# Field loads of a pairwise product kernel, divided between two queues and chosen DMA engines

## Chip, cores and metric

The kernel runs on one core of a Trainium2 chip. The metric is the device time in microseconds (us) of one execution. A core has five engines that matter here: TensorE (PE, matrix products; its weight loads are shown as PEld), VectorE (DVE), ScalarE (ACT), GpSimd (POOL) and SyncE (SP), which only issues transfers. Transfers between the chip's memory (HBM) and the core's own memory are carried out by 16 DMA engines. They are issued by SyncE, ScalarE or GpSimd, each on a queue of its own.

## Reference

There are 32 fields of 128 numbers for each of 1024 samples. For each of the 496 pairs of fields i < j, the vector of field i is multiplied by a 128 x 128 matrix of the pair's own, and the product is multiplied element by element with the vector of field j. All is in 32-bit floats.

```python
v_i = inputs[:, I_IDX, :]                       # (1024, 496, 128)
v_j = inputs[:, J_IDX, :]
transformed = jnp.einsum('bpd,ped->bpe', v_i, W)   # W: (496, 128, 128)
return transformed * v_j
```

The inputs are 16.8 MB of fields and 32.5 MB of matrices, the output is 260 MB.

## Kernel before

The host lays the fields out as `xt[128, 32, 1024]` (one row per component) and the matrices as `wt[62, 128, 8, 128]`, eight pairs to a 512 KB piece. A step `u` is one half (512 samples) of one pair `q`. Pairs go by falling i, so that the first ones need few fields. For the first 15 pairs TensorE multiplies the 32-bit floats as they are; for all later ones both factors are split into three parts (high, low, a difference), made by ScalarE and GpSimd, and three faster products are added. VectorE multiplies the result in PSUM by field j and writes it into an output tile `ot` of four pairs (2 MB), of which there are three.

```python
def load_x(f, n=1, pieces=1, eng=None):
    ...
        t = xpool.tile([P, n, BT], F32, tag=f"x{f}", name=f"x_{f}")   # one buffer per field
    ...
        (eng or nc.sync).dma_start(out=t[:, :, k * s : (k + 1) * s], in_=xt[:, f : f + n, k * s : (k + 1) * s])

def split_w(c, u):                    # two pairs' matrices
    ...
    nc.scalar.mul(h, raw, 1.0 - 2.0**-13)                               # wh, ScalarE
    nc.gpsimd.tensor_tensor(l, raw, h.bitcast(F32), ALU.subtract)       # wl
    nc.gpsimd.tensor_scalar(d, h.bitcast(F32), EPS, 1.0, ALU.mult, ALU.mult)
    nc.gpsimd.tensor_tensor(d, l.bitcast(F32), d.bitcast(F32), ALU.subtract)   # wd

# split_x does the same for half a field (xh, xl, xd)

# before the loop: matrices 0 to 2 and fields 31 to 24 are loaded
load_w(0, (0, 1, WL), nc.sync)
load_x(NF - 2, pieces=2, eng=nc.scalar)
load_x(NF - 1, pieces=2, eng=nc.scalar)
load_x(NF - 3)
load_x(NF - 4)
load_w(1, eng=nc.sync)
for f in range(NF - 5, NF - 4 - XLEAD, -1):
    load_x(f)
load_w(2, eng=nc.sync)
...
for u in range(2 * NQ + LAG + SLAG):
    q = u // 2
    if u < 2 * NQ:
        i, j = pairs[q]
        if u % 2 == 0 and j == i + 1 and 0 < i - 2 - XLEAD:
            load_x(i - 2 - XLEAD)              # at the first pair of field i: field i - 7
        first(u)                               # two products, ScalarE scales
        if u % 2 == 1 and q in w_at:
            load_w(w_at[q])
        if u == 2 * x_at + 1:
            load_x(0)
    if LAG <= u < 2 * NQ + LAG:
        second(u - LAG)                        # third product, VectorE writes ot
    while stores and stores[0][0] <= u - LAG:
        nc.scalar.dma_start(*stores.pop(0)[1:])
    ...                                        # split_w, split_x when due
```

Each engine works through its instructions in the order in which they are written here. Fields 23 to 1 are loaded inside the loop, all of them by SyncE.

Of the kernel before, what the change touches and what calls it, by code (L numbers as in the profile page):

```python
# [7 lines left out]
F32 = mybir.dt.float32  # L8
# [3 lines left out]
P = 128  # L12
NF = 32
NQ = NF * (NF - 1) // 2
BT = 1024
# [10 lines left out]
WLEAD = 12  # L26
XAFTER = 54
XLEAD = 5
SLAG = 2


# [6 lines left out]
def kernel(  # L38
# [22 lines left out]
    nc = tc.nc  # L61
# [3 lines left out]
    xpool = ctx.enter_context(tc.tile_pool(name="x", bufs=1))  # L65
# [6 lines left out]
    x_sb = {}  # L72

    def load_x(f, n=1, pieces=1, eng=None):

        if f == 0:

            t = rpool.tile([P, WL, P], F32, tag="w", name="x_0").rearrange("p q e -> p (q e)").unsqueeze(1)
        else:
            t = xpool.tile([P, n, BT], F32, tag=f"x{f}", name=f"x_{f}")  # L80
        s = BT // pieces
        for k in range(pieces):
            (eng or nc.sync).dma_start(out=t[:, :, k * s : (k + 1) * s], in_=xt[:, f : f + n, k * s : (k + 1) * s])
        for k in range(n):
            x_sb[f + k] = t[:, k, :]

    w_raw = {}

    def load_w(c, splits=(0, WL), eng=nc.sync):
        w_raw[c] = rpool.tile([P, WL, P], F32, tag="w", name=f"w_{c}")  # L90
        for a, b in zip(splits, splits[1:]):
            eng.dma_start(out=w_raw[c][:, a:b, :], in_=wt[c, :, a:b, :])
# [42 lines left out]
            todo.append((first_q[i + 1] + 1 if i < NF - 3 - NATIVE else 2, first_q[i], lambda u, i=i, a=a: split_x(i, a, u)))  # L135
    todo.sort(key=lambda t: t[1])

    load_w(0, (0, 1, WL), nc.sync)
    load_x(NF - 2, pieces=2, eng=nc.scalar)
    load_x(NF - 1, pieces=2, eng=nc.scalar)  # L140
# [8 lines that stand above are left out]
# [13 lines left out]
    def first(u):  # L162
        q, h = divmod(u, 2)
        i, c = pairs[q][0], q // WC
        r = slice(q % WC * P, (q % WC + 1) * P)
        s = slice(h * HB, (h + 1) * HB)
        po[u] = ppool.tile([P, HB], F32, tag="po", name=f"po_{u}")
        if q < nq0:
            nc.tensor.matmul(po[u], w_raw[q // WL][:, q % WL, :], x_sb[i][:, s], start=True, stop=True)  # L169
        else:  # L170
            for t in (0, 1):
                nc.tensor.matmul(po[u], w_s[c][t][:, r], x_s[i][t][:, s], start=t == 0, stop=t == 1)  # L172
            nc.scalar.mul(po[u], po[u], 1.0 + EPS)  # L173

    def second(u):
        q, h = divmod(u, 2)
        i, j = pairs[q]
        r = slice(q % WC * P, (q % WC + 1) * P)
        s = slice(h * HB, (h + 1) * HB)
        if q >= nq0:  # L180
            nc.tensor.matmul(  # L181
                po[u], w_s[q // WC][2][:, r], x_s[i][2][:, s], start=False, stop=True, skip_group_check=True
            )
        g, k = divmod(q, OG)
        if k == 0 and h == 0:
            ots[g] = opool.tile([P, OG, BT], F32, tag="ot", name=f"ot_{g}")
        nc.vector.tensor_tensor(ots[g][:, k, s], po.pop(u), x_sb[j][:, s], ALU.mult)  # L187
        if q >= NQ - 2:
            stores.append((u + SLAG, out[g, :, k, s], ots[g][:, k, s]))
        elif g == 0 or q >= NQ - OG:  # L190
            if h == 1:
                stores.append((u + SLAG, out[g, :, k], ots[g][:, k]))
        elif k == OG - 1 and h == 1:
            stores.append((u + SLAG, out[g], ots[g]))

    for u in range(2 * NQ + LAG + SLAG):
        q = u // 2
        if u < 2 * NQ:
            i, j = pairs[q]
            if u % 2 == 0 and j == i + 1 and 0 < i - 2 - XLEAD:  # L200
                load_x(i - 2 - XLEAD)
            first(u)
            if u % 2 == 1 and q in w_at:
                load_w(w_at[q])
# [3 lines that stand above are left out]
            second(u - LAG)  # L208
        while stores and stores[0][0] <= u - LAG:
            nc.scalar.dma_start(*stores.pop(0)[1:])  # L210
        if u % 2 == 1:
            ready = [t for t in todo if t[0] <= q]
            if ready:
                ready[0][2](u)
                todo.remove(ready[0])
        while later and later[0][0] <= u:
            nc.vector.tensor_tensor(*later.pop(0)[1:], ALU.subtract)  # L217
    assert not todo and not later and not stores


# [25 lines left out]
```

## Time and profile before

| | |
|---|---|
| time, median of 3 runs | 755.02 us (754.97 to 755.28) |
| span of the profiled execution | 753.2 us |
| stores, 2 MB each | 122, 12.5 us from issue to landing |
| matrix loads, 512 KB each | 61, 10.3 us |
| field loads by SyncE, 512 KB each | 30, 16.0 us |
| HBM read, written | 49.28 MB, 260.05 MB |

A page of the profile begins with the busy time of each engine and its share of the span, and the number of its instructions. Then come 40 equal slices of the span; the row DMA is the mean busy share of the 16 DMA engines in tenths, and GB/s is what they moved. For each queue the page has packets, MB and the time of its packets as a share of 16 engines' span. A row of a group of instructions has line, engine, operation, what it writes and reads, the count, then busy us and mean ns of one, then the idle time of the engine before them and what ended it. A row of waits reads: engine and line, what it waited for, us in total, times, longest us. The trace has besides every DMA packet with start, duration and size, though not the DMA engine that carried it, and the time of every increment of a transfer's semaphore, sixteen for each transfer.

### The profile page before, as it was taken

To read this page: it belongs to the slowest core of one execution; us is meant where nothing else is said; L and a number is where in the kernel's file an instruction comes from. 1 tells how busy PE (TensorE), PEld (TensorE's weight loads), DVE (VectorE), ACT (ScalarE), POOL (GpSimd) and SP (SyncE) were. 2 spreads that over 40 slices of the span, in tenths; PEclk is the share of its full clock that TensorE was granted. 3 is DMA by queue.
4 is the path that set the end of the run, shared out by engine and by line. 5 is a ranking of instruction groups with operands and counts; after the bars stand their busy time and mean duration, and the time that the engine had idled before them with its cause. 6 is when DMAs were issued, how large, how long until landed. Compare 5 with 4: busy or idle time off the path is not lost.

```text
span 753.2 us, 10948 instructions
## 1 busy us (share of the span) xinstructions
PE 706.5 (94%) x2946; PEld 546.0 (72%) x2946; DVE 624.1 (83%) x1012; ACT 627.1 (83%) x1256; POOL 595.5 (79%) x863
## 2 busy tenths in 40 slices
PE   7989999999999999999999999999999999999993
PEld 3567776777777777777777778777777777777782
DVE  4989888888887878888878897988888889888894
ACT  1389888889988898888888889898989898988892
POOL 1788998888988987978879797888887879796660
PEclk9999999999999999999999999999999999999997
DMA  9999999999999999999999999999999999999997
GB/s 353 428 427 423 430 427 424 423 417 433 399 425 406 411 420 413 415 405 401 425 401 422 412 401 422 400 432 405 417 419 421 399 432 401 425 406 413 425 397 312
DMA packets 33038, 310.04 MB, mean 412 GB/s; under 512 B 3665, under 2 KB 3793, under 8 KB 17361
## 3 DMA queue, kind: packets, MB, share of 16 engines
q10 hardware_dynamic: 19584, 261.10, 82.5%
q1 hardware_dynamic: 13392, 48.24, 16.8%
q8 instruction: 24, 0.39, 0.2%
q14 instruction: 38, 0.30, 0.1%
HBM read 49.28 MB, written 260.05 MB: 411 GB/s over the span
## 4 chain that ended last, share of the span: by engine, by line
DMA 43%; PE 32%; DVE 13%; POOL 6%; ACT 2%; issue 2%; DVEq 0%; ACTq 0%; POOLq 0%
DMA out_dram<-ot 42%; PE po L172 19%; DVE ot L187 12%; PE po L181 9%; PE po L169 4%; ACT po L173 2%; POOL xd L122 2%; POOL wl L102 1%; POOL xl L117 1%; POOL wd L104 1%; ACT wh L101 1%; POOL xl L118 1%; POOL wd L103 0%; DVE xd L217 0%; DMA x<-in_xt_dram 0%
## 5 line engine op out<-in xcount | busy, mean ns | idle before, releaser
L187 DVE TENSOR_TENSOR ot<-po,x 128x512 f32<-128x512 f32 x992 | 610.1, 682 | 118.5 <-DMA out_dram<-ot 50.7
L173 ACT ACTIVATE po<-po 128x512 f32<-128x512 f32 x962 | 543.4, 583 | 94.3 <-PE po L172 41.0
L172 PE MATMUL po<-xh,wh 128*128 128x512 f32 x962 | 382.8, 398 | 21.4 <-DVE ot L187 20.5
L172 PE MATMUL po<-xl,wl 128*128 128x512 f32 x962 | 376.6, 392 | 4.8 <-POOL wl L102 4.8
L181 PE MATMUL po<-xd,wd 128*128 128x512 f32 x962 | 375.2, 390 | 4.0 <-DVE xd L217 3.4
L172 PEld LDWEIGHTS po<-xh,wh 128*128 128x128 f32 x962 | 180.4, 188 | 88.8 <-DVE ot L187 50.8
L102 POOL TENSOR_TENSOR wl<-w,wh 128x256 fp32r<-128x256 f32 x241 | 178.3, 740 | 73.3 <-ACT wh L101 71.8
L181 PEld LDWEIGHTS po<-xd,wd 128*128 128x128 f32 x962 | 180.6, 188 | 44.0 <-ACT po L173 4.7
L172 PEld LDWEIGHTS po<-xl,wl 128*128 128x128 f32 x962 | 180.7, 188 | 42.2 <-POOL wl L102 8.8
L104 POOL TENSOR_TENSOR wd<-wl,wd 128x256 fp32r<-128x256 f32 x241 | 180.5, 749 | 20.1
L103 POOL TENSOR_SCALAR wd<-wh 128x256 fp32r<-128x256 f32 x241 | 101.3, 420 | 20.3
L101 ACT ACTIVATE wh<-w 128x256 fp32r<-128x256 f32 x241 | 99.5, 413 | 5.1 <-DVE ot L187 3.3
L117 POOL TENSOR_TENSOR xl<-x,xh 128x512 fp32r<-128x512 f32 x52 | 67.2, 1292 | 18.1 <-ACT xh L116 17.7
L122 POOL TENSOR_TENSOR xd<-xh,xl 128x512 fp32r<-128x512 f32 x32 | 41.4, 1294 | 2.7
L116 ACT ACTIVATE xh<-x 128x512 fp32r<-128x512 f32 x52 | 32.5, 629 | 11.3 <-DMA x<-in_xt_dram 11.2
L118 POOL TENSOR_SCALAR xl<-xl 128x512 fp32r<-128x512 f32 x52 | 33.7, 649 | 4.6
L169 PE MATMUL po<-x,w 128*128 128x512 f32 x60 | 27.8, 623 | 4.4 <-DMA x<-in_xt_dram 4.3
L169 PEld LDWEIGHTS po<-x,w 128*128 128x128 f32 x60 | 11.6, 198 | 19.8 <-issue 12.3
L217 DVE TENSOR_TENSOR xd<-xh,xl 128x512 fp32r<-128x512 f32 x20 | 17.2, 859 | 0.0
L116 ACT ACT_TABLE_LOAD x1 | 1.3, 1283 | 2.6 <-issue 2.6
L233 POOL MEMSET const-float32-0.0<- 128x1 f32 x1 | 0.1, 98 | 0.2 <-issue 0.2
L233 POOL MEMSET const-bfloat16-1.0<- 128x1 bf16 x1 | 0.1, 101 | 0.0
(2 smaller groups left out, 0.2 us busy)
## 6 DMA issues: line engine op xcount, KB each, us to landing
out_dram<-ot ACTq DMA_DIRECT2D x122, 2048.0 KB, 12.5
w<-in_wt_dram SPq DMA_DIRECT2D x61, 512.0 KB, 10.3
x<-in_xt_dram SPq DMA_DIRECT2D x30, 512.0 KB, 16.0
out_dram<-ot ACTq DMA_DIRECT2D x6, 512.0 KB, 9.2
x<-in_xt_dram ACTq DMA_DIRECT2D x4, 256.0 KB, 5.9
out_dram<-ot ACTq DMA_DIRECT2D x4, 256.0 KB, 8.2
w<-in_wt_dram SPq DMA_DIRECT2D x1, 448.0 KB, 4.7
w<-in_wt_dram SPq DMA_DIRECT2D x1, 64.0 KB, 2.9
```

The lines of the kernel that those rows point to most:

```text
L101: nc.scalar.mul(h, raw, 1.0 - 2.0**-13)
L102: nc.gpsimd.tensor_tensor(l, raw, h.bitcast(F32), ALU.subtract)
L103: nc.gpsimd.tensor_scalar(d, h.bitcast(F32), EPS, 1.0, ALU.mult, ALU.mult)
L104: nc.gpsimd.tensor_tensor(d, l.bitcast(F32), d.bitcast(F32), ALU.subtract)
L117: nc.gpsimd.tensor_tensor(l, x_sb[f][:, s], h.bitcast(F32), ALU.subtract)
L118: nc.gpsimd.tensor_scalar(l, l.bitcast(F32), 1.0 / EPS, 1.0, ALU.mult, ALU.mult)
L122: nc.gpsimd.tensor_tensor(d, h.bitcast(F32), l.bitcast(F32), ALU.subtract)
L169: nc.tensor.matmul(po[u], w_raw[q // WL][:, q % WL, :], x_sb[i][:, s], start=True, stop=True)
L172: nc.tensor.matmul(po[u], w_s[c][t][:, r], x_s[i][t][:, s], start=t == 0, stop=t == 1)
L173: nc.scalar.mul(po[u], po[u], 1.0 + EPS)
L181: nc.tensor.matmul(po[u], w_s[q // WC][2][:, r], x_s[i][2][:, s], start=False, stop=True, skip_group_check=True)
L187: nc.vector.tensor_tensor(ots[g][:, k, s], po.pop(u), x_sb[j][:, s], ALU.mult)
```

## The change

Fields 23 to 1 are no longer loaded by one transfer of SyncE over all 16 DMA engines. GpSimd issues a transfer of 104 rows, arranged so that it falls on 13 DMA engines with 8 rows each; SyncE issues the other 24 rows, arranged for two engines (odd fields) or twelve (even fields). The host reorders the rows of these fields to suit. Small transfers into a tile `mark`, which nothing reads, move the position at which GpSimd's next transfer begins: one of four engines at the start, one of three after each field (13 + 3 = 16), one of twelve at the end. The aim is to choose which DMA engines carry the later fields, so that some carry fewer of them. The scratch memory for GpSimd's descriptors grows from 256 to 2048.

```diff
+XROWS = 104
+BY_TWO = range(1, NF - 3 - XLEAD, 2)
...
+    mark = xpool.tile([32, 16], F32, tag="mark", name="mark")
+
+    def move_on(k):
+        nc.gpsimd.dma_start(out=mark[: 2 * k], in_=xt[: 2 * k, 0, :16].rearrange("(b a) n -> a b n", a=k))
+
+    def load_x_apart(f):
+        t = xpool.tile([P, BT], F32, tag=f"x{f}", name=f"x_{f}")
+        nc.gpsimd.dma_start(out=t[:XROWS], in_=xt[:XROWS, f, :].rearrange("(b a) n -> a b n", a=13))
+        rest = xt[XROWS:, f, :]
+        if f in BY_TWO:
+            rest = rest.rearrange("(b a) n -> a b n", a=2)
+        nc.sync.dma_start(out=t[XROWS:], in_=rest)
+        x_sb[f] = t
+        move_on(3)
...
+    move_on(4)
     load_w(0, (0, 1, WL), nc.sync)
...
             if u % 2 == 0 and j == i + 1 and 0 < i - 2 - XLEAD:
-                load_x(i - 2 - XLEAD)
+                load_x_apart(i - 2 - XLEAD)
...
             nc.vector.tensor_tensor(*later.pop(0)[1:], ALU.subtract)
+    move_on(12)
...
+    for f in range(1, NF - 3 - XLEAD):
+        xt[:XROWS, f] = xt[:XROWS, f].reshape(13, 8, BT).transpose(1, 0, 2).reshape(XROWS, BT).copy()
+        if f in BY_TWO:
+            xt[XROWS:, f] = xt[XROWS:, f].reshape(2, 12, BT).transpose(1, 0, 2).reshape(P - XROWS, BT).copy()
...
-    nc = _bacc.Bacc("TRN2", ..., dynamic_dma_scratch_size=256)
+    nc = _bacc.Bacc("TRN2", ..., dynamic_dma_scratch_size=2048)
```

More of the change, by code (lines that the diff above doesn't have):

```diff
@@ L230 @@
     xt = _np.ascontiguousarray(x.transpose(2, 1, 0))
+    for f in range(1, NF - 3 - XLEAD):
+        xt[:XROWS, f] = xt[:XROWS, f].reshape(13, 8, BT).transpose(1, 0, 2).reshape(XROWS, BT).copy()
+        if f in BY_TWO:
+            xt[XROWS:, f] = xt[XROWS:, f].reshape(2, 12, BT).transpose(1, 0, 2).reshape(P - XROWS, BT).copy()
     wt = _np.ascontiguousarray(w[perm].reshape(NQ // WL, WL, P, P).transpose(0, 3, 1, 2))
-    nc = _bacc.Bacc("TRN2", target_bir_lowering=False, num_devices=1, dynamic_dma_scratch_size=256)
+    nc = _bacc.Bacc("TRN2", target_bir_lowering=False, num_devices=1, dynamic_dma_scratch_size=2048)
     arrays, args = {}, []
```

## Prediction

> **What bounds the kernel now.** I read the page first: busy shares, then the slices and the queues.
>
> ```profile
> span 753.2 us, 10948 instructions
> PE 706.5 (94%) x2946; PEld 546.0 (72%) x2946; DVE 624.1 (83%) x1012; ACT 627.1 (83%) x1256; POOL 595.5 (79%) x863
> ...
> DMA  9999999999999999999999999999999999999997
> GB/s 353 428 427 423 430 427 424 423 417 433 399 425 406 411 420 413 415 405 401 425 401 422 412 401 422 400 432 405 417 419 421 399 432 401 425 406 413 425 397 312
> ...
> q10 hardware_dynamic: 19584, 261.10, 82.5%
> q1 hardware_dynamic: 13392, 48.24, 16.8%
> ```
>
> PE has the highest share, but the DMA row is full in every slice but the last. 310 MB are moved, 261 MB of them by the queue of ScalarE (the stores) and 48 MB by that of SyncE (weights and fields). The speed is the thing to see: about 427 GB/s in slices 1 to 9 (20 to 190 us), then mostly 400 to 425. The windows say the same:
>
> ```profile
> core 0: us, PE busy (x) PEld busy (x) DVE busy (x) ACT busy (x) POOL busy (x), PEclk, DMA share, GB/s
> 40.00:100.00 60.00, 54.98 (x234) 42.88 (x233) 52.62 (x84) 52.14 (x107) 53.67 (x73) 1.00 1.01 427
> 100.00:140.00 40.00, 37.11 (x154) 27.94 (x155) 33.78 (x56) 33.44 (x70) 35.47 (x50) 1.00 1.01 427
> 140.00:200.00 60.00, 57.09 (x241) 44.23 (x240) 51.65 (x85) 51.70 (x106) 51.88 (x75) 1.00 1.01 414
> ...
> 320.00:384.00 64.00, 60.89 (x260) 47.96 (x260) 52.68 (x88) 55.72 (x112) 53.26 (x79) 1.00 1.00 407
> ```
>
> The engines are all busy, yet they move less after 140 us. The packet records say why. A 16 KB packet takes 611 ns in 13,398 of 15,616 cases, and the next one starts 4 ns before it ends: 16384 B / 607 ns = 27.0 GB/s, times 16 = 432 GB/s, so the first 140 us run at the ceiling. The sixteen semaphore increments of each store show the rest. In the stores issued from 15 to 60 us the fifteenth comes 12.26 us after issue and the sixteenth 12.59 (medians). From 384 to 740 us the eighth comes after 7.5 us, the fifteenth after 8.8, the sixteenth after 12.0. One engine of sixteen is late. Following packets back from those last increments gives an engine that never pauses and whose 16 KB packets take 635 ns in the mean and 4 KB packets 168 instead of 159: 4% slower than its neighbours. It falls behind until the three output buffers are used up, at about 140 us, and from there sets the pace. Its neighbours then show stretched packets (up to over 1 us); counted above 611 and 159 ns they come to 8.3 us per engine from 140 to 384 us and 10.9 from 384 to 740. I take most of this as neighbours run dry and starting again.
>
> The waits name the same buffers, and one more line matters for this change:
>
> ```profile
> POOL wl L102 <- ACT wh L101: 71.8, 99, 2.8
> PEld po L172 <- DVE ot L187: 50.8, 79, 1.2
> DVE ot L187 <- DMA out_dram<-ot: 50.7, 58, 1.8
> ...
> PEld po L172 <- POOL wl L102: 8.8, 10, 1.2
> ```
>
> DVE waits 50.7 us for a store to free its buffer, nearly all after 140 us. GpSimd's 79% hides a tight first half. Its groups from 60 to 100 us:
>
> ```profile
> L104 POOL TENSOR_TENSOR wd<-wl,wd 128x256 fp32r<-128x256 f32 x13 | 10.1, 773 | 1.1
> L102 POOL TENSOR_TENSOR wl<-w,wh 128x256 fp32r<-128x256 f32 x13 | 9.9, 763 | 0.5
> L117 POOL TENSOR_TENSOR xl<-x,xh 128x512 fp32r<-128x512 f32 x6 | 7.8, 1297 | 0.0
> L103 POOL TENSOR_SCALAR wd<-wh 128x256 fp32r<-128x256 f32 x13 | 6.4, 493 | 1.1
> L118 POOL TENSOR_SCALAR xl<-xl 128x512 fp32r<-128x512 f32 x6 | 4.3, 713 | 0.5
> ```
>
> The idle column is only the 80 ns between two instructions: it waits for nothing. Gaps over 0.12 us sum to 5.6 us from 20 to 60, to 0 from 60 to 120, and to 18.7 us from 140 to 384. The split weights are ready only 0.3 to 5.9 us before TensorE wants them (0.8 us near 102).
>
> **What the Trainium skill says.** "DMA: Bandwidth & Descriptors", section "Latency and other measured facts", says that DMA engines 7 and 15 are usually slower than the others, with a cause only guessed. The trace before agrees that one engine is slower, by 4%; it doesn't tell its number. The same page, "Why a DMA increments its semaphore by 16 and not by 1": a transfer uses the largest k up to 16 that divides the outer sizes of both sides; SyncE's and ScalarE's transfers take the k lowest engines, GpSimd's take k consecutive ones from a cursor that goes round, and GpSimd's transfers post an increment from all 16 engines whatever their k. No run yet shows GpSimd's part, as the kernel before issues nothing from it. The first section gives about 1 us to the first byte of a GpSimd transfer against 0.6 from SyncE. "Perfetto Trace Analysis", "DMA Instruction — SWDGE (GPSIMD)": the descriptors are written by GpSimd's own processors, so the issue is time on POOL; not shown by this trace either.
>
> **The change part by part.** 23 fields (23 down to 1), each 512 KB, or 8 rows of 4 KB per engine, are loaded apart.
>
> Rows per engine. Before: 23 x 8 = 184. GpSimd's 104 rows are 13 engines x 8. The first mark (four engines) and each mark of three move the cursor so that the same three engines are always left out. SyncE's 24 rows go to two engines (12 rows each, 12 odd fields) or twelve (2 rows each, 11 even fields): 166 rows on the two lowest engines, 22 on the next ten. The plan adds up if the two lowest and the slow engine are the three left out: then the slow one has 0 or 22 rows, the two 166, those with both shares 206, the rest 184. The slow engine loses 162 to 184 packets x 164 ns = 27 to 30 us; nine or ten others gain 22 x 155 ns = 3.4 us.
>
> But fields are loaded only in the first half: the last of the 23 was issued at 379 us. From 140 to 384 us the neighbours' 8.3 us can come back, less the 3.4: -5. From 384 on the slow engine has its full load again: 63 stores x 8 x 631 ns + 33 loads x 8 x 164 ns = 318 + 43 = 361 us, which is what that part takes now. It starts that part without its lag, and the lag (3 us behind the fifteenth engine, 4.5 behind the eighth) is all that is won there: about -5. So at best -10.
>
> What GpSimd pays. Per field two issues: I estimate 1.0 us for 104 rows and 0.7 for the small mark, from the skill's 1 us to first byte. At 1.7 us per field:
> - Up to 60 us: some seven fields, 12 us, of which the first three fall into its idle 15 us at the start. The other four cost 7, against 5.6 of room. All marks write one tile, so each waits for the one before to land, whose increments stand behind 8 field packets per engine: 8 x (611 + 159 + 159) = 7.4 us when the queues are full. The fields from 20 down follow each other after 2 to 6 us of GpSimd's work, so I add up to 8 us of waiting there. Less 4 us of lead: PE loses about 5.
> - 60 to 140: five fields, 8.5 us, and no room: +8.
> - DMA meanwhile works off the field loads that are queued (they land 20 us after issue there), worth -4 later.
> - 140 to 384: eleven fields x 1.7 = 18.7 us, all the room there is. GpSimd then bounds this part, and the 5 us of relief are not collected: 0.
>
> Sum: +5 + 8 - 4 + 0 - 5 = +4. With some chance that the marks cost less than this, 755.0 + 3 = 758 us.
>
> **The rivals.** (1) The issues are cheap, say 0.4 us a field: GpSimd keeps its room, DMA stays the bound, and both reliefs come: 755 - 10 + 2 = about 747. For it: the first half is bound by DMA on every view. Against: 60 to 120 us has no gap at all. (2) The issues are dear, 2.5 us a field: 23 x 0.8 us more than assumed, 18 us, in parts where GpSimd has no room: about 776. (3) The position is not where the plan wants it. If the three left out are 1, 2 and 3, engine 0 gets 184 + 166 = 350 rows, 166 x 155 ns = 26 us more, in the first half alone: a new straggler, some 15 us after the lag that the buffers absorb, about 770. Against it: 13 + 3 and the two lowest engines fit too well to be unmeasured. (4) The loads were hidden anyway and GpSimd has slack elsewhere: no change, 755.
>
> **Range and chances.** The main number is one I have no measurement of, GpSimd's time per issue: 0.1 us per field is 1.5 to 2 us of the whole. From rival 1 to rival 2 gives 746 to 775. Faster by over 2% would be under 740, more than both reliefs together: 0.02. Slower by over 2% is over 770, rivals 2 and 3: 0.14. The rest: 0.84.
>
> **What would show it.** Right: issue instructions on POOL of 0.7 to 1 us, 47 in all; PE waiting for POOL's wl or wd between 30 and 140 us; the sixteenth increment of stores beside the fifteenth up to 384 us, and 3 us late again from about 540; DVE's wait for stores below 50.7 us. Wrong: if issues are short, POOL's waits for ACT stay and the time falls under 750. If another engine trails in the first half, the position was missed. If the late engine trails as before although it has no field rows, my reading of the lag is wrong.

## Result and profile after

The changed kernel takes 780.5 us in the median of 6 runs (778.7 to 781.6), the kernel before 755.0 (755.0 to 755.3): ratio 1.0334, 95% interval 1.032 to 1.0349. The prediction was 758 with a range of 746 to 775: it missed by 22 us, and the time lies outside its range.

The page of the kernel after, the same rows as were shown of before:

```profile
span 777.5 us, 11026 instructions
...
PE 709.9 (91%) x2946; PEld 551.7 (71%) x2946; DVE 643.0 (83%) x1012; ACT 627.8 (81%) x1256; POOL 623.5 (80%) x911
...
DMA  9979999999999999999999999999999999999998
GB/s 280 371 298 391 376 357 422 388 425 413 402 390 408 417 418 418 424 416 411 402 411 400 382 411 412 399 425 400 428 394 431 418 409 418 419 407 410 414 408 330
...
q10 hardware_dynamic: 19584, 261.10, 80.9%
q1 hardware_dynamic: 10788, 38.44, 13.6%
q0 software_dynamic: 4112, 9.82, 3.9%
```

GpSimd's queue q0 has taken 9.8 MB from SyncE's q1. The loss is at the start: the first six slices move 280, 371, 298, 391, 376 and 357 GB/s, where before had 353 and then 423 to 430. The windows sharpen it (columns as in the prediction). Those of after:

```profile
0.00:20.00 20.00, 14.34 (x25) 5.74 (x26) 6.85 (x12) 1.28 (x1) 3.20 (x9) 1.00 0.92 284
20.00:40.00 20.00, 17.26 (x41) 7.23 (x39) 12.39 (x20) 4.83 (x10) 13.41 (x16) 1.00 1.02 374
40.00:60.00 20.00, 12.96 (x48) 10.20 (x49) 11.63 (x19) 9.97 (x20) 11.33 (x19) 0.75 0.78 290
...
100.00:140.00 40.00, 34.99 (x150) 27.67 (x150) 36.83 (x55) 33.09 (x67) 37.12 (x54) 1.00 0.98 385
140.00:200.00 60.00, 55.93 (x242) 44.56 (x240) 56.07 (x88) 52.88 (x108) 55.62 (x79) 1.00 1.01 414
320.00:384.00 64.00, 60.63 (x257) 47.24 (x256) 51.35 (x85) 55.17 (x111) 55.61 (x82) 1.00 1.01 413
```

And those of the first 60 us of before:

```profile
0.00:20.00 20.00, 15.63 (x33) 6.43 (x34) 9.83 (x15) 4.00 (x6) 4.12 (x8) 1.00 0.91 356
20.00:40.00 20.00, 20.00 (x65) 11.91 (x64) 18.63 (x29) 7.86 (x17) 15.00 (x22) 1.00 1.03 428
40.00:60.00 20.00, 17.38 (x73) 13.18 (x72) 16.64 (x27) 16.25 (x34) 16.76 (x23) 1.00 1.01 426
```

In the first 40 us the transfers are busy (0.92 and 1.02) and yet move less: packets are stretched. From 40 to 60 us they are not even busy (0.78): TensorE works 12.96 us in place of 17.38, and little is there to store. So two different things happen.

I compare kernels below by **delay**: the start of VectorE's product of step u, less its start in the kernel before. For after it is 6.7 us at step 20 (27 us into the span of before), 14.1 at step 30, 14.0 at 40, 18.4 at 80 (74 us), 18.7 at 160 (137 us), 22.6 at 480 (378 us), 23.9 at 560 and 25.3 at the end. So 18 of the 25 us are lost before 92 us of after's own span, about five between 137 and 437 us, and nothing is won back later.

Waits of the kernel after (engine and line, what it waited for, total us, times, longest):

```profile
DVE ot L211 <- DMA out_dram<-ot: 54.9, 49, 2.8
PEld po L196 <- POOL wl L125: 41.4, 27, 7.1
...
PE po L196 <- POOL wl L125: 30.8, 23, 6.8
...
POOL mark L99 <- DMA mark<-in_xt_dram: 21.6, 5, 8.1
ACT xh L139 <- DMA x<-in_xt_dram: 18.1, 2, 17.3
```

TensorE's weight loads now wait 41.4 us for GpSimd's `wl`, where they waited 8.8. GpSimd waits 21.6 us for its own marks. VectorE waits for the stores a little longer than before (54.9 against 50.7), where a relief of the slow engine should have shortened this. The timeline of GpSimd shows the worst of the marks (start, duration, instruction, idle time before it):

```profile
36.24 0.64 POOL L104 DMA_DIRECT2D x<-in_xt_dram  x1
44.96 0.56 POOL L99 DMA_DIRECT2D mark<-in_xt_dram  x1 [8.08 <-DMA mark<-in_xt_dram]
45.53 0.73 POOL L125 TENSOR_TENSOR wl<-w,wh 128x256 fp32r<-128x256 f32 x1
```

and that of TensorE takes it over:

```profile
46.32 0.79 PE L196 MATMUL po<-xl,wl 128*128 128x512 f32 x1 [6.75 <-POOL wl L125]
```

The mark could not be issued until the mark before it had landed. `wl` stood behind it in GpSimd's order, and TensorE behind `wl`. Last, GpSimd's groups from 60 to 100 us, with the two kinds of issue:

```profile
L125 POOL TENSOR_TENSOR wl<-w,wh 128x256 fp32r<-128x256 f32 x12 | 9.4, 781 | 0.5
...
L104 POOL DMA_DIRECT2D x<-in_xt_dram x3 | 1.9, 638 | 0.0
L99 POOL DMA_DIRECT2D mark<-in_xt_dram x3 | 1.7, 567 | 0.0
```

638 + 567 ns, 1.2 us per field, where I had put 1.7.

Each store posts sixteen semaphore increments. Medians in us after the issue of the 8th, the 15th and the 16th, and the median of how far the last trails the one before, worked out from the trace:

```
stores issued from   before                   after
60 to 140 us         10.5  12.0  13.2  1.4     8.1   9.2  10.2  0.7
140 to 260            8.4   9.8  12.9  3.0     9.4  10.5  11.3  0.3
260 to 384            8.2  10.5  13.0  2.5     8.3  12.0  12.4  0.4
430 to 500            7.8   8.9  11.6  2.6     7.5   9.6  11.9  2.2
500 to 740            7.4   8.6  12.0  3.2     7.6   9.2  11.9  2.9
```

The 16th stands beside the 15th up to 384 us, as the prediction asked. But from 140 us on the 15th has become later, which a slow engine that has been relieved doesn't explain: another engine trails too.

### The profile page after: what moved, and what is told of

Its sections match the earlier page's. It is cut to its first block, busy times and chain, and to the rows that moved or that the text cites. A ratio compares the mean times of both kernels' runs of the same rounds, so it can differ in the third digit from the quotient of the medians.

```text
span 777.5 us, 11026 instructions
## 1 busy us (share of the span) xinstructions
PE 709.9 (91%) x2946; PEld 551.7 (71%) x2946; DVE 643.0 (83%) x1012; ACT 627.8 (81%) x1256; POOL 623.5 (80%) x911
## 3 DMA queue, kind: packets, MB, share of 16 engines
q1 hardware_dynamic: 10788, 38.44, 13.6%
## 4 chain that ended last, share of the span: by engine, by line
PE 42%; DMA 27%; POOL 19%; DVE 6%; issue 4%; ACT 2%; DVEq 0%; POOLq 0%; SPq 0%; ACTq 0%
PE po L196 28%; DMA out_dram<-ot 23%; PE po L205 13%; DVE ot L211 5%; POOL xl L140 5%; POOL wl L125 4%; POOL xd L145 3%; POOL wd L127 3%; POOL xl L141 3%; DMA x<-in_xt_dram 2%; POOL wd L126 2%; DMA mark<-in_xt_dram 1%; ACT po L197 1%; ACT wh L124 1%; DMA w<-in_wt_dram 1%
## 5 line engine op out<-in xcount | busy, mean ns | idle before, releaser
L211 DVE TENSOR_TENSOR ot<-po,x 128x512 f32<-128x512 f32 x992 | 627.0, 684 | 119.7 <-DMA out_dram<-ot 54.9
L196 PE MATMUL po<-xl,wl 128*128 128x512 f32 x962 | 380.7, 396 | 34.9 <-POOL wl L125 30.8
L196 PEld LDWEIGHTS po<-xl,wl 128*128 128x128 f32 x962 | 181.8, 189 | 82.5 <-POOL wl L125 41.4
L125 POOL TENSOR_TENSOR wl<-w,wh 128x256 fp32r<-128x256 f32 x241 | 181.1, 751 | 58.7 <-ACT wh L124 57.3
L126 POOL TENSOR_SCALAR wd<-wh 128x256 fp32r<-128x256 f32 x241 | 99.1, 411 | 20.5
L193 PE MATMUL po<-x,w 128*128 128x512 f32 x60 | 30.2, 660 | 6.3 <-DMA x<-in_xt_dram 5.7
L99 POOL DMA_DIRECT2D mark<-in_xt_dram x25 | 14.5, 580 | 22.5 <-DMA mark<-in_xt_dram 21.6
L241 DVE TENSOR_TENSOR xd<-xh,xl 128x512 fp32r<-128x512 f32 x20 | 18.4, 921 | 5.3 <-POOL xl L141 5.2
L104 POOL DMA_DIRECT2D x<-in_xt_dram x23 | 14.7, 637 | 0.1
```

## Experiments

All times are medians, and each ratio is to runs of the kernel before on the same chip. Kernels that are compared with each other ran in part on different chips; the kernel before took 755.0 to 755.3 us on each. Two theories stood at first: GpSimd's time and waits (marks, issues) against the transfers themselves (which engine carries what, and in which order).

### Marks, and an overloaded engine

**Each mark its own tile**, so that none waits for another:

```diff
-    mark = xpool.tile([32, 16], F32, tag="mark", name="mark")
+        mark = xpool.tile([32, 16], F32, tag=f"mark{len(marks)}", name="mark")   # in move_on
```

> The kernel after, but every mark is written into a tile of its own, so that no mark waits for the one before. Theory W (the waits of the marks on each other, 21.6 us in the profile, are most of the 25 us): about 762 us. Theory I (GpSimd's time for issuing, 1.2 us per field, in a stretch without room, is most): 775 us or more. Theory S (the first fields on GpSimd's queue go ahead of the loads that the start needs): no better than 778 us, as two or three of them now go out even earlier.

781.02 us, 1.0341 (1.0323 to 1.0358): no gain. The marks' waits are gone, and the delay at step 40 falls from 14.0 to 9.2, but it grows back to 25.0 by step 480. The wait that took the place:

```profile
DVE ot L213 <- DMA out_dram<-ot: 82.4, 62, 4.0
```

The last increment of a store now comes 3.5 to 5 us after the 15th from early on, up to about 430 us. This looks like one overloaded engine, and the next runs ask which.

**Another starting position.** The first mark over two or six engines in place of four (and the last over 14 or 10):

```diff
-    move_on(4)
+    move_on(2)      # in the other kernel move_on(6)
```

> The kernel after with the first mark over two engines in place of four and the last over fourteen, so that GpSimd's 13 engines begin two places lower. Theory P with the position at 0 when the kernel begins: the 13 are engines 2 to 14, and 15, 0 and 1 are left out; no engine has more than 206 rows: 757 to 764 us. If the position at the beginning is another, one of the two lowest stays in and it is 775 us or more. Theory G: 778 us.

> The kernel after with the first mark over six engines and the last over ten, so that the 13 begin two places higher. Theory P with position 0: engines 6 to 15, 0, 1 and 2; both of the two lowest now have 350 rows: 778 to 785 us, as one such engine already set the pace. Theory G: 780 us too, so this run tells only together with the one that begins two lower.

Beginning two lower: 773.57 us, 1.0247 (1.0232 to 1.0262). Two higher: 785.53, 1.0401 (1.038 to 1.0422). **SyncE's 24 rows always over twelve**, `BY_TWO = ()`, so that no engine gets 12 of them:

> The kernel after, but SyncE's 24 rows go over twelve engines for odd fields too, none over two; all else stays, GpSimd's issues and waits included. Theory P (the 13 engines include the lowest one, which so carries 184 + 166 = 350 rows of field, 26 us more than in the kernel before, and sets the pace): that engine now has 184 + 46 = 230 rows, 7 us more, so 760 to 766 us. Theory G (GpSimd's waits and issues and the early field loads): no change, 778 us or more.

776.07 us, 1.0279 (1.0262 to 1.0296). All three agree with a starting position of 0: then the 13 engines of after are 4 to 15 and 0, those left out are 1, 2 and 3, and engine 0, one of SyncE's two lowest, carries 23 x 8 + 166 = 350 rows. Two lower leaves out 15, 0 and 1, and nobody is overloaded; two higher leaves out 3, 4 and 5, and both lowest are. The first and the third were expected at 757 to 764 and at 760 to 766 us, and came out some 10 us slower: other losses stayed, which the runs further below find. In after's trace, following one engine's packets back through the field load issued at 98.5 us, 8 rows of GpSimd's and 12 of SyncE's are found on the same engine; the increments of SyncE's two engines come 11.1 and 14.5 us after issue.

**Both remedies together**, the position two lower and marks apart:

> The kernel after with both changes: GpSimd's 13 engines begin two places lower (which took 7 us off), and every mark has a tile of its own (which took nothing off while one engine was overloaded). If the marks' waits count once no engine is overloaded: 765 to 768 us, the loss by step 30 falling from 13.5 to 7 us. If they don't count at all: 773 us.

765.52 us, 1.0139 (1.0124 to 1.0154). The overload can be seen to go in SyncE's loads over two engines: with marks apart and one engine overloaded, one of the two posts its increment 9.5 us after issue and the other 20.4 (medians of twelve loads); here it is 11.1 and 13.6. With the others this run makes a square:

```
                              marks wait     marks apart
one engine with 350 rows        780.5           781.0
no engine overloaded            773.6           765.5
```

The overload costs 15.5 us where the marks don't wait and 7 where they do; the marks cost 8 where nothing is overloaded and nothing where something is. I read this as two losses that hide each other: while the marks hold TensorE up, the overloaded engine works off its rows.

### What GpSimd's issues cost alone

The kernel before, with two small GpSimd transfers at each later field (16 rows of 64 B, into 16 tiles in turn; none waits for another) and the fields left with SyncE:

```diff
                 load_x(i - 2 - XLEAD)
+                small()          # two nc.gpsimd.dma_start(out=mark[:16], in_=xt[:16, 0, :16])
```

> The kernel before, with two small transfers (16 rows of 64 bytes) issued by GpSimd beside each of the 23 later field loads, which stay whole on SyncE. It measures GpSimd's issue time alone, with no mark waiting for another and no field on GpSimd's queue. Theory I: 770 us or more. Theories W and S: 755 to 763 us; 46 issues of 0.57 us are 26 us, of which some 20 fall behind 40 us and meet about 20 us of room.

757.44 us, 1.0031 (1.0019 to 1.0043): 2.4 us for 46 issues. GpSimd's full row from 60 to 120 us made it look like the bound there; it was not, as the delay is only 0.7 at step 80 and 1.2 at step 160.

### The start

**Only fields 16 to 1 divided**, 23 to 17 whole by SyncE as before:

```diff
+APART = 17
-                load_x_apart(i - 2 - XLEAD)
+                (load_x_apart if i - 2 - XLEAD < APART else load_x)(i - 2 - XLEAD)
```

> The kernel after, but the first seven later fields (23 to 17) are loaded as in the kernel before, and only fields 16 to 1 are divided. Theories W and S put the loss into the first 60 us: 755 to 763 us. Theory I: 16 of 23 fields still pay their issue where GpSimd has no room, about 770 us. If a missed position costs time by itself, the excess over 755 us stays through the middle of the run.

763.64 us, 1.0108 (1.0091 to 1.0125). The delay is 1.0 at step 160, so the first 137 us are healed, and then grows to 9.2 at step 480: the 16 fields' share of the overloaded engine, in clean surroundings. **Only fields 23 and 22 whole** (`APART = 22`):

> The kernel after, but fields 23 and 22, whose divided loads go out at 2 and 8 us ahead of loads that the start needs, are loaded as in the kernel before. If their going first is what the start loses: no delay at step 20 (6.7 us in the kernel after), and 770 to 773 us in all. If the waits between the marks of fields 20 to 18 matter more: 776 us or more.

771.7 us, 1.0224 (1.0209 to 1.024), 8.8 less than after. At step 20 the delay is 1.1 in place of 6.7. The timeline of GpSimd in after shows why those two matter:

```profile
2.14 0.60 POOL L104 DMA_DIRECT2D x<-in_xt_dram  x1
7.16 0.55 POOL L99 DMA_DIRECT2D mark<-in_xt_dram  x1 [4.42 <-DMA mark<-in_xt_dram]
7.71 0.58 POOL L104 DMA_DIRECT2D x<-in_xt_dram  x1
```

GpSimd has nothing to do at the start and issues fields 23 and 22 at 2.1 and 7.7 us, beside the fields that are needed first and that stand in SyncE's queue. The 4 KB packets of the first 20 us: in after 257 ns in the mean on GpSimd's queue and 204 on SyncE's, 284 GB/s in all; in before 164 ns and 356 GB/s; with the two fields whole 165 ns and 355, as this window shows:

```profile
0.00:20.00 20.00, 15.78 (x32) 6.63 (x33) 9.80 (x14) 4.00 (x6) 5.00 (x10) 1.00 0.92 355
```

The field that SyncE issues at 4.6 us lands at 18.6 us in after, at 12.5 in before and with the two fields whole.

**Is it the arrangement of the rows?** The kernel before with every later field read in strides (each engine every 16th row), in one transfer of SyncE's:

```diff
-        load_x(f)
+        nc.sync.dma_start(out=t, in_=xt[:, f, :].rearrange("(b a) n -> a b n", a=16))   # host reorders to suit
```

> The kernel before, with fields 23 to 1 loaded by SyncE in one transfer over all 16 engines as before, but each engine reads every 16th row. Theory A: stretched packets from 10 us on and 760 to 767 us. Theory Q: one queue, so packets of 159 ns and 755 us.

757.01 us, 1.0025 (1.0015 to 1.0034): strides alone cost 2 us. **Rows in order** in the changed kernel, `"(a b) n -> a b n"` for both parts:

> The kernel after, but each of the 13 engines (and each of the two) reads rows that follow each other in memory, 8a to 8a+7, where the kernel after has every 13th row; engines, queues, waits and bytes stay. Theory A (the arrangement of rows makes the engines read the same part of memory in step, which stretches the 4 KB packets of field loads to 250 ns in the first 20 us): the packets go back to about 160 ns and half of the early loss of 14 us goes, 768 to 773 us. Theory Q (two queues that read fields at the same time stretch them): no change, 778 us or more.

769.34 us, 1.0187 (1.0172 to 1.0202). This is no clean test: rows in order merge to one dimension, SyncE's 24 rows then always went over twelve, and over how many engines GpSimd's 104 went I can't tell. Against the kernel with 24 rows always over twelve it wins 6.7 us, with packets of 215 ns in place of 263 on GpSimd's queue in the first 20 us. So strides and two queues together do more harm than strides alone; the parts are not separated.

**The division by SyncE alone**: before, with 120 rows (15 engines) and 8 rows as two transfers of SyncE's:

```diff
+        nc.sync.dma_start(out=t[:120], in_=xt[:120, f, :])
+        nc.sync.dma_start(out=t[120:], in_=xt[120:, f, :])
```

> The kernel before, with each of the 23 later fields loaded by SyncE as 120 rows (15 lowest engines) and 8 rows (8 lowest engines), GpSimd issuing nothing. If the slow engine is the highest one, it is relieved of all 184 rows without GpSimd's cost: 745 to 750 us, and no late sixteenth increment before 384 us. If it is another engine: 755 to 760 us, with the lag as before.

765.26 us, 1.0134 (1.0119 to 1.0149), 8 of the 10 us between steps 40 and 60, without any work on GpSimd. In 40 to 60 us its 4 KB packets take 227 ns (before 161), and ScalarE, which issues the stores, is held up once in this way:

```profile
ACT po L180 <- DMA x<-in_xt_dram: 6.2, 1, 6.2
```

The trace shows how: each transfer takes one of a few semaphores in turn and waits until it is free. The store issued at 58.0 us waits for the semaphore of the field load issued at 36.8. One more transfer per field shifts the turn. Whether this wait makes up the whole 8 us was not separated from the longer packets. This kernel also keeps the later fields off the highest engine (120 rows post 15 + 1 increments, 8 rows 8 + 1), and the last increment still trails by 2.6 us from 140 to 260 and 2.8 from 260 to 384: that engine is not the slow one.

### Which engine is slow

**A series of lone loads** after the work of the kernel before: eight 16 KB rows per engine, over 16, 15, ... 2 engines by SyncE, then over three by GpSimd, one after another.

```diff
+    for k in range(16, 1, -1):
+        nc.sync.dma_start(out=t[: 8 * k], in_=flat[: 8 * k].rearrange("(b a) n -> a b n", a=k))
+    for _ in range(16):
+        nc.gpsimd.dma_start(out=t[:24], in_=flat[:24].rearrange("(b a) n -> a b n", a=3))
```

> The kernel before, and when all is stored a series of loads one after the other, each of which waits for the one before: by SyncE 8 rows of 16 KB for each of k engines, k from 16 down to 2; then sixteen by GpSimd of 8 such rows for each of three engines, which walk three places at a time. Work is added, so the total (some 950 us) says nothing. The slow engine shows packets of about 635 ns. If it is number s, SyncE's loads have them for k over s only; GpSimd's have them in the loads that cover it, which gives its place from where GpSimd begins: with position 0 those t for which s is 3t, 3t+1 or 3t+2 modulo 16. From the run with 120 rows the slow one is not number 15; by theory P, a4 and the rows of the after kernel I expect it in 4 to 14.

1044.64 us with the added work, and no answer: with three engines of GpSimd's at a time 18 to 21 of the 24 packets of a load took 608 to 613 ns, wherever they began, and the few others up to 1.8 us. The slow engine did not show itself when few engines read.

**Thirteen, walking.** Fields 16 to 1 divided as 104 rows by GpSimd and 24 by SyncE over twelve, the rest as before, and no marks: each load begins where the last ended (13 on), and the load over all evens out.

```diff
-                load_x(i - 2 - XLEAD)
+                (load_x_apart if i - 2 - XLEAD < 17 else load_x)(i - 2 - XLEAD)   # without move_on
```

> Fields 16 to 1 alone are divided (104 rows over 13 engines by GpSimd, 24 over twelve by SyncE), and there are no marks: the 13 engines begin 13 places further with every field, so the three left out walk through all 16 in six fields. In the field loads whose 13 include the slow engine about 8 of GpSimd's 104 packets take 161 to 182 ns, in those that leave it out next to none: that gives its number, counted from where GpSimd begins. If it is between 4 and 14, as the packets of the earlier runs say, neither the kernel after nor the one that begins two lower ever relieved it. Time: 757 to 761 us, as the load is even and the slow engine loses 3 rows of 16 on average.

757.23 us, 1.0028 (1.0016 to 1.004). The division itself is thus nearly free. Followed back from the late increments, the engine with 635 ns packets carries rows of GpSimd's in thirteen of the sixteen loads. The three others were issued at 98.8, 220.8 and 362.9 us, the 4th, 10th and 15th; from position 0 they leave out engines 4 to 6, 2 to 4 and 3 to 5. Number 4 alone is in all three. After leaves out 1 to 3: it misses by one. The kernel that begins two higher leaves out 3 to 5 and so this engine too, but overloads both of SyncE's lowest (785.5 us). Followed in the same way through after, the engine with 635 ns packets carries rows of GpSimd's in 15 of the 16 loads issued from 73 us on: it was not relieved.

**The test.** Fields 16 to 1 as 112 rows over 14 engines by GpSimd and 16 rows over 16 by SyncE, marks of two in own tiles. Left out are engines 7 and 8 in one kernel, 4 and 5 in the other:

```diff
+    move_on(9)      # leaves out 7 and 8; in the other kernel move_on(6): 4 and 5
...
+        nc.gpsimd.dma_start(out=t[:112], in_=xt[:112, f, :].rearrange("(b a) n -> a b n", a=14))
+        nc.sync.dma_start(out=t[112:], in_=xt[112:, f, :])
+        move_on(2)
```

> Fields 16 to 1 are divided into 112 rows on 14 engines by GpSimd, beginning at 9, so that with position 0 engines 7 and 8 are left out, and 16 rows by SyncE, one for each engine; marks (of two engines) have tiles of their own. If the slow engine is 7 (the skill's page names 7 and 15, and 15 is excluded) it has 16 rows instead of 128: no late sixteenth increment until 430 us, 750 to 755 us. If it is another: the lag stays, 757 to 760 us.

> As e2_skip_seven_eight (fields 16 to 1 as 112 rows over 14 engines, 16 rows over 16, own marks), but GpSimd begins at 6, so that the two engines left out are nos. 4 and 5 from its position and not 7 and 8. Theory: the slow engine is no. 4, and its relief brings back some of the lag: seven rows of 16 fields less, 112 x 164 ns = 18 us less to move on it, so the 16th increment of a store lands within 0.5 us of the 15th up to about 430 us, and the time is 751 to 757. Rival 1: the relief is seen in the landings but the lag was not what bounds, 757 to 760 as e2 (759.3). Rival 2: no. 4 is not the slow one, the lag of the 16th increment stays 1 to 3 us, 759.

With 7 and 8 left out 759.3 us, 1.0053 (1.0036 to 1.007). With 4 and 5 left out **751.44 us, 0.9948 (0.9937 to 0.996)**, faster than before and after, and 7.9 us faster than the same transfers on other engines. (The two ran on different chips; before took 755.1 us on both.) The list of waits shows it in VectorE's wait for stores. With 7 and 8 left out:

```profile
DVE ot L214 <- DMA out_dram<-ot: 53.3, 59, 2.7
```

With 4 and 5 left out, the same line:

```profile
DVE ot L214 <- DMA out_dram<-ot: 19.8, 23, 1.9
```

How far the 16th increment trails the 15th (medians, us):

```
stores issued from   before   7, 8 left out   4, 5 left out   matrices too, 4, 5   matrices too, 12, 13
140 to 260 us          3.0          0.2             0.2               0.2                   1.4
260 to 384             2.5          2.9             0.4               0.3                   4.0
430 to 500             2.6          3.4             0.6               0.4                   2.7
500 to 740             3.2          3.1             0.9               0.4                   1.7
```

That the last engine in the middle column trails only from 260 us on I can't explain; the column beside it differs in nothing but the two engines. With 7 and 8 left out the engine with 635 ns packets carries 4 to 11 rows of GpSimd's in each of the sixteen loads (a full share is 8; the following is not exact); with 4 and 5 left out it can be followed from 215 us on, and there it has two at most. The windows from 140 to 384 and 384 to 740 us of before:

```profile
140.00:384.00 244.00, 230.42 (x975) 179.99 (x974) 200.64 (x330) 210.95 (x424) 208.55 (x300) 1.00 1.01 413
384.00:740.00 356.00, 347.27 (x1492) 276.54 (x1491) 306.00 (x499) 318.23 (x636) 278.74 (x415) 1.00 1.00 413
```

and of the kernel with 4 and 5 left out of the fields:

```profile
140.00:384.00 244.00, 226.71 (x978) 183.35 (x977) 221.19 (x331) 211.52 (x427) 221.49 (x321) 0.99 1.01 418
384.00:740.00 356.00, 343.41 (x1497) 279.49 (x1495) 329.64 (x502) 318.94 (x637) 280.93 (x420) 1.00 1.00 418
```

413 GB/s become 418 in both. Counted above 611 ns for 16 KB and 159 for 4 KB, what the packets take longer falls from 8.2 to 5.9 us per engine in the first of these windows and from 10.7 to 6.6 in the second. I take this as the neighbours that no longer run dry; it agrees with it and does not prove it.

**More relief**: also every second matrix load from no. 36 on (13 loads) over the same 14 engines; the same with 12 and 13 left out; and matrices alone, every second from no. 8 on (27 loads), no field divided.

```diff
+W_APART = range(36, 62, 2)      # alone: range(8, 62, 2), and no field apart
+        nc.gpsimd.dma_start(out=t[:112], in_=s[:112].rearrange("(b a) n -> a b n", a=14))   # matrix c
+        nc.sync.dma_start(out=t[112:], in_=s[112:])
+        move_on(2)
```

> f1_skip_four_five, and also every second matrix load from no. 36 on (13 loads) as 112 rows by GpSimd over the same 14 engines with 16 rows by SyncE over 16. Theory: the slow engine's excess, 4% of some 750 us or about 29 us, is then fully taken away (29 loads x 7 rows x 164 ns = 33 us), the lag of the 16th increment stays under 0.7 us to the end, and the time is 745 to 753. Rival 1: relief does not pay, 758 to 762, with 13 x 1.2 us more of issues on GpSimd hidden or not.

> f2_fields_and_matrices with GpSimd beginning at 14, so that nos. 12 and 13 are left out instead of 4 and 5: the same transfers and issues, the wrong engines. Theory: the slow engine now carries 9 rows of each divided load instead of 8, the lag is as before or larger, 760 to 768. Rival 1 (which engines are left out does not matter): within 1.5 us of f2.

> The kernel before with no field divided; every second matrix load from no. 8 on (27 loads) as 112 rows by GpSimd over 14 engines from 6 (4 and 5 left out), 16 rows by SyncE over 16, marks of 2. Theory: relief of the slow engine over the whole run without touching the fields' stretch beyond it, 27 x 7 x 164 ns = 31 us off no. 4: the lag stays under 1 us, 744 to 752. Rival 1: relief does not pay, 756 to 760.

In this order: 757.93 us (1.003, 1.0017 to 1.0044), 763.26 (1.0111, 1.0097 to 1.0126) and 756.8 (1.0009, 0.9996 to 1.0023). The first and the third miss what was expected of them (745 to 753 and 744 to 752): their rival, that more relief does not pay, fits. The right pair against the wrong one is again worth 5.3 us, and with it the lag is gone to the end. But dividing the matrices as well costs more than it brings: 6.5 us slower than the fields alone. The windows from 384 to 740 us, of fields and matrices with 4 and 5 left out:

```profile
384.00:740.00 356.00, 341.64 (x1489) 278.78 (x1487) 328.27 (x497) 316.86 (x634) 294.90 (x443) 1.00 1.00 413
```

It is back at 413 GB/s, and its packets take 11.7 us per engine longer, although no engine trails. The runs of the first and third of these kernels also spread more than any other (753 to 762 and 751 to 758 us), and the trace of the first is of its fastest run, 753.2 us: it wins 3.5 us against before up to step 640 and loses nearly all of it by step 900. What stretches the packets there was not found.

## Why the prediction was wrong

**The bound** was read rightly: DMA, with one slow engine that sets the pace from 140 us on. The relief works when it reaches that engine: 7.9 us between two kernels that differ in nothing but the engines left out, and 3.7 against before.

**The step that failed first** is "The plan adds up if the two lowest and the slow engine are the three left out", together with the rejection of rival 3 because "13 + 3 and the two lowest engines fit too well to be unmeasured". The three left out are 1, 2 and 3. The slow engine, no. 4, keeps GpSimd's 8 rows of every field, and engine 0 gets 350 rows. The prediction's own sign for this came true, another engine that trails in the first half: from 15 to 60 us the last increment of a store trails by 2.4 us, before by 0.2. Rival 3 had even the rows and the cost right: about 15 us, measured 15.5 where the marks don't cover it. How much the buffers absorb was not worked out there, so part of this is luck. Its total, 770, lacked what follows.

**A term that was missing** is the start. I counted GpSimd's time for the first three fields as free, since it is idle there, and it is. I did not ask where their transfers go: ahead of the fields that TensorE waits for, with stretched packets. That is 6.7 us at step 20 (1.1 with those two fields whole), and that kernel is 8.8 us faster in all, though it also takes two fields' share off the overloaded engine.

**The marks' waiting** was right in kind and nearly in size. I had worked out 7.4 us for one mark behind eight field packets in full queues, the longest was 8.1, and taking them away wins 8.05 us where no engine is overloaded. I let PE lose "about 5" to this and the early issues.

**The issues** were mis-sized: 1.7 us per field estimated, 1.2 measured. More than that, "60 to 140: five fields, 8.5 us, and no room: +8" is wrong as a step. 46 issues alone cost 2.4 us in all, and 1.5 us of delay between steps 60 and 160, which the kernel before does from 58 to 137 us. GpSimd without a gap was not the bound there.

**"140 to 384: 0"**, because GpSimd would bind, is wrong too. This part follows the transfers. After loses 3.9 us in it (delay 18.7 at step 160, 22.6 at 480). With fields 16 to 1 alone divided the loss is about 8 us with the overloaded engine, 1.9 with even load, and 0.7 us are won with the right pair left out.

**"From 384 on: about -5"** could not be seen in after, which enters that part with the lag still building (2.2 us at 430 to 500). With the right pair left out the lag stays small to the end, and the delay goes from -0.8 at step 480 to -3.6: 2.8 us, half of the estimate. (Its working has 33 loads after 384 us where 29 are issued, which takes 5 us off the 361.)

So the sum 5 + 8 - 4 + 0 - 5 should have read: overload and marks 15.0 together, start 6 to 7, issues 2.4, and no relief, which is 23 to 24 of the 25.5 us measured; the parts come from separate kernels, so that they add up is no proof. One of the prediction's signs held though its cause did not: the 16th increment beside the 15th up to 384 us. The slow engine was not relieved; from 260 to 384 us it is the 15th that came later (12.0 for 10.5 us) more than the 16th that came earlier (12.4 for 13.0). TensorE's waits for `wl` held with their cause, and VectorE's wait for stores, asked to fall below 50.7 us, rose to 54.9.

## What to carry to other kernels

A plan that leaves out chosen DMA engines stands on a position that must be measured: leave out each of several groups with the same transfers and look at the last increments. Here the wrong group cost 4.2 us and the right one won 3.7. Before moving loads to an idle queue, ask what they will overtake at the start, and let no issue on a computing engine wait for another transfer to land. When two losses overlap, remove them one at a time and together; removing one may show nothing.

## What was not expected

- The Trainium skill ("DMA: Bandwidth & Descriptors", "Latency and other measured facts") names engines 7 and 15 as usually slower. Here it is the one counted as 4 from GpSimd's first position: leaving out 4 and 5 cuts the lag of the last increment (0.9 us from 500 to 740), leaving out 7 and 8 doesn't (3.1), nor does sparing SyncE's highest. It was found on one chip and relieved on another; why it is slow no run shows.
- That engine takes 635 ns for 16 KB packets where the others take 611, in the kernel's own traffic. Lone loads over three engines at a time, which cover all sixteen, show 611 in most packets. Whether it is the load or something else that brings the 24 ns out was not tested.
- The lone loads of 16 KB rows, consecutive rows 128 KB apart, took 611 ns a packet over up to four engines and 1219 to 1256 over eight to fifteen (medians). What limits this was not followed.
- The same page's "Why a DMA increments its semaphore by 16 and not by 1" held in all that could be seen: GpSimd's transfers over 13 engines post 16 increments, SyncE's 24 rows over two post 2 + 1 and over twelve 12 + 1.
